# Two fused attention layers over eight images: units moved within layers, sums copied first at the end, and a copy given to another engine

## The chip, the cores and the metric

One core of one Trainium2 chip runs the kernel. The metric is the device time of one execution in microseconds (us); the figure for a kernel is the median of its runs. A profiled execution is one of its own, with a time of its own; its span is the stretch that the hardware profiler records.

The engines named below: TensorE (PE) multiplies matrices and writes into PSUM, VectorE (DVE) adds and multiplies element by element, ScalarE (ACT) computes exponentials and copies, GpSimd (POOL) does small work, and SyncE (SP) issues most DMAs. PSUM has eight banks; one bank holds 128 partitions by 512 floats here.

## The reference, cut to what matters

```python
# x: 8 images, 64 channels, 64 x 64 positions (n = 4096)
# layer 0
f = Wf @ x + bf            # 8 rows
g = Wg @ x + bg            # 8 rows
hh = Wh @ x + bh           # 64 rows
s = einsum('bci,bcj->bij', f, g)
o = einsum('bcj,bij->bci', hh, softmax(s, axis=2))
x = x + o
# layer 1
xn = group_norm(x, gamma, beta)            # 8 groups of 8 channels
q, k, v = split(w_qkv @ xn + b_qkv, 3)
attn = softmax(q.T @ k * 64 ** -0.5)
x = x + w_proj @ (attn @ v.T).T + b_proj
```

Both layers are full attention over 4096 positions, for each of eight images, in 32-bit floats.

## The kernel before, in words

**Tiling.** The 4096 positions of an image are taken as two halves of 2048, which lie on partitions 0 to 63 and 64 to 127. The queries of both halves are worked in four chunks of 512 columns (`NC`, `CW`). For each chunk the keys go by in 16 tiles (`NT`); one key tile of one chunk is a *step*. A step makes the scores of the queries against two groups of 128 keys, the exponentials of these, and two jobs on the exponentials: PE *weighs* the values with them, adding into an accumulator in PSUM, and DVE adds them up elementwise into `esum`, for the divisor of the softmax. In the trace those sums are the rows `TENSOR_TENSOR esum_l<-esum_l,e_l 128x2048`, or with `kq_l`, `vt_l` or `free` in the place of `esum_l` where the sum is kept elsewhere. The first sum of a chunk joins the tiles of the chunk's first two steps (`e_l,e_l`). The exponentials stand in a ring of seven buffers (`e`, `ppool`).

**Order of the layers.** `L0(0), L0(1), L1(0), L0(2), L1(1), ..., L0(7), L1(6), L1(7)`, where L0(b) is layer 0 of image b: layer 1 of an image runs after layer 0 of the next image. Layer 0 has scores of few rows (8 channels, split into a high and a low part), so it takes PE least of all against DVE; layer 1 needs more of PE.

**PSUM.** Banks 1 to 6 are three pairs for scores. Banks 0 and 7 are accumulators: layer 0 uses one of the two for a chunk, by turns (chunks 0 and 2 bank 0, chunks 1 and 3 bank 7), layer 1 both. In layer 0 PE goes in *rounds*: it scores six banks full, or seven when the accumulator that isn't in use is free (bank 0 is then the first of the seven, bank 7 the last), or two fewer when a pair is lent to a *unit*; ACT takes the exponentials, and PE meanwhile weighs the exponentials of the round before.

**Units.** All work beside scoring, weighing and summing is cut into units: projections (`project`, `project_direct`, `project_all`), values (`values`), normalisation (`normal`), and what follows a chunk (`finish`). `at_step(s, work, takes)` puts a unit down for step s, and `take` hands out those that are due, at most one at a time of those that need a pair of banks (`PAIR`) or a bank (`BANK`). The due steps of `before()` count from the start of the preceding layer 1, or for image 0's layer 1 from the start of layer 0 of image 1 (step 64, the `where` of line 861). So a unit of image 0's layer 1 with due step under 64 is done in layer 0 of image 1, and from 64 on in layer 1 of image 0 itself.

**When a chunk is done.** `finish` has its accumulator copied out of PSUM into `raw` by `total`: by one copy on ACT in layer 0 (L664); in layer 1 by two copies on ACT, or by a copy and a sum on DVE where layer 0 comes next. Then come, as units, `halves` (the sum of the two key groups of `esum`), `transposed` (the DVE reduction `part_l`), `reciprocals`, and `result` with `residual`. For chunks 0 to 2 of layer 0 of images 1 to 7 the sums are held until layer 1 of another image runs (`holds`). The very last chunk has its own ending, `end` (L434): the sums by PE into a bank, their reciprocal `rt` (L456), a copy of them `zs_end` (L458), the copy of one accumulator to `raw_end` (L460), the sum with the other, the check of all sums against `SUM_MIN` and `SUM_MAX` (`ok_end`, `bad`), the residual, and two stores of the output (L817). Were a sum of exponentials out of bounds, a general path would run; with these inputs it doesn't.

**Order on the engines.** Every matmul goes through `matmul` (L150, recorded at L151), which chains it behind the one before: PE's order is the order of the program. DVE's operations go through `InOrder` (L138, recorded at L141); they are chained only while `tight` is set, which is during the first eight chunks and in `end`. Otherwise the scheduler of the Tile framework places the operations of DVE and ACT. `behind` holds a unit until the latest sum of exponentials has been issued.

**The start.** `warm(ones, 18)` and `warm(wfg, 10)` give PE matmuls of no use while the first data come (L194, L236). The small weights WfT and WgT come by two DMAs each, by ACT's and SP's queue (L196 to L198), then x of image 0 by SP (L199); GpSimd's queue brings the biases, and GpSimd makes `lane` (iota), `fgb` and others. `project_direct` makes f and g of chunk 0, `project(0, (1,))` those of chunk 1, `project(1)` those of chunks 2 and 3: PE, then ACT adds the bias (`full`, L586), then DVE parts f and g into a high and a low part (`high`, `split`), then 8 or 16 small DMAs by SP lay the parts out on the partitions (L602).

Of the kernel before, what the change touches and what calls it, by code (L numbers as in the profile page):

```python
# [9 lines left out]
F32 = mybir.dt.float32  # L10
F32R = mybir.dt.float32r
# [8 lines left out]
CW = 512  # L20
P = 128
# [47 lines left out]
def fast_path(  # L69
# [125 lines left out]
    w1 = const.tile([P, 2, C8], F32, name="w1")  # L195
    for i, (w, queue) in enumerate(((WfT, nc.scalar), (WgT, nc.sync))):  # L196
        for h in range(2):
            queue.dma_start(w1[ts(h, C), i, :], w)  # L198
# [36 lines left out]
    wfg = wfg.rearrange("p i s c -> p (i s c)")  # L235
    warm(wfg, 10)  # L236
    fgb_low = const.tile([P, 2], F32, name="fgb_low")
# [95 lines left out]
    class Attention:  # L333
# [100 lines left out]
        def end(self, acc, esum, e, t):  # L434
# [18 lines left out]
            for p in range(2):  # L453
                self.weigh(acc, e[:, p], t, p, False, p == 1, slice(0, CW))
            rt = work.tile([P, width], F32, tag="zs", name="rt")
            vector.reciprocal(rt, z)  # L456
            zs = work.tile([P, width], F32, tag="zs", name="zs_end")
            nc.scalar.copy(zs, z)  # L458
            raw = work.tile([P, CW], F32, tag="raw", bufs=4, name="raw_end")
            nc.scalar.copy(raw, acc[0])  # L460
            vector.tensor_add(raw, acc[1], raw)
            for rows, (h, i) in zip(groups, parts):
                matmul(
                    laid[ts(h, C), i, :],
                    ident[rows, rows.start : rows.start + 1].broadcast_to([32, C]), rt[rows, :],
                    start=True, stop=True, tile_position=(rows.start, h * C),
                )
            by_half = raw.rearrange("p (i n) -> p i n", i=2)
            vector.tensor_mul(by_half, by_half, laid)
            for k in range(2):  # L470
# [7 lines left out]
                bad[:, 1:], dealt, SUM_MAX, ok, op0=ALU.is_le, op1=ALU.mult  # L478
            )
            for i in range(1 + QP):  # L480
                matmul(bad_ps, bad[:, i : i + 1], ones[:, 0:1], start=i == 0, stop=i == QP)
# [3 lines left out]
    class Layer0(Attention):  # L485
# [4 lines left out]
        def before(self):  # L490
# [3 lines left out]
            def begin():  # L494
# [78 lines left out]
        def project(self, k, js=(0, 1)):  # L573
# [4 lines left out]
            for j in js:  # L578
# [84 lines left out]
        def total(self, raw, acc, index):  # L663
            nc.scalar.copy(raw, acc[0])  # L664
            return None
# [6 lines left out]
    class Layer1(Attention):  # L672
# [8 lines left out]
        def before(self):  # L681
# [130 lines left out]
        def residual(self, o, c):  # L812
            vector.scalar_tensor_tensor(
                o, o, k1["pb"], x_tiles[self.b][:, ts(c, CW)], op0=ALU.add, op1=ALU.add
            )
            for h in range(2):
                nc.sync.dma_start(out[self.b, :, ds(h * NH + c * CW, CW)], o[ts(h, C), :])  # L817
            if c == NC - 1 and self.b + 3 < B:
                load_x(self.b + 3)
# [607 lines left out]
```

## Time and profile before

| | us |
|---|---|
| median of 10 runs | 2988.5 |
| lowest and highest of them | 2987.9, 2991.91 |
| the profiled execution | 2988.05 |
| its span | 2986.2 |
| PE's granted clock in the span, of full speed | 0.999 |

The profiled execution is 1.85 us longer than its span. By stretch of the trace, with the busy time of the three engines that matter:

| stretch (us from the start of the span) | what runs | PE | DVE | ACT |
|---|---|---|---|---|
| 545.5 to 691 | L0(2) | 145.09 | 139.68 | 122.02 |
| 691 to 914 | L1(1) | 223.00 | 182.30 | 135.86 |
| 914 to 1059 | L0(3) | 144.59 | 139.55 | 121.91 |

A busy time is the time in which an engine had some operation going. A line of the timeline gives the start of an operation, its length, the engine, the line of the code, and `out<-in` with the tile names; `x7` at its end says that seven alike were drawn together, and what stands in brackets is the idle time just before and who ended it. Line 141 is the helper for all of DVE's operations and line 151 that for all of PE's, so they are told apart by tile. In a row of the costliest groups, the numbers behind the bar are busy time, the mean of one in ns, and the idle time before them.

The end of the kernel, from the timeline: the sums are read by DVE's reciprocal first, then by ACT.

```profile
2974.30 1.76 DVE L141 RECIPROCAL rt<-banks 128x256 f32<-128x256 f32 x1 [0.81 <-PE banks L151]
...
2976.10 0.37 ACT L458 COPY zs_end<-banks 128x256 f32<-128x256 f32 x1 [3.86 <-DVE rt L141]
...
2976.37 0.59 ACT L460 COPY raw_end<-banks 128x512 f32<-128x512 f32 x1
...
2978.66 0.74 DVE L141 SCALAR_TENSOR_TENSOR raw_end<-raw_end,pb,x 128x512 f32<-128x512 f32 x1
```

### The profile page before, as it was taken

The numbers are of one execution on the slowest core, as the hardware profiler recorded it, in microseconds if no ns is written. First come the engines' busy times: TensorE is split into PE (matmuls) and PEld (weight loads), VectorE is DVE, ScalarE is ACT, GpSimd is POOL, SyncE is SP. The second block draws the span as 40 slices with busy tenths as digits, with TensorE's granted clock in tenths as the row PEclk, the third lists the DMA queues.
The fourth block names the chain that finished last, engine by engine and source line by source line (L and its number), as shares of the span: only waits on it lengthen the run. The fifth ranks groups of instructions, "written<-read, shape, count | busy, mean of one in ns | idle before, by whom it ended". The sixth has DMA issues, their size and how long they took to land.

```text
span 2986.2 us, 58391 instructions
## 1 busy us (share of the span) xinstructions
PE 2969.5 (99%) x25693; PEld 1080.6 (36%) x25693; DVE 2567.8 (86%) x1634; ACT 2072.4 (69%) x2019; POOL 16.1 (1%) x40
## 2 busy tenths in 40 slices
PE   9999999999999999999999999999999999999998
PEld 4333333333333333333333333333333333333333
DVE  7999986899869998799977999769997699976776
ACT  7888666786667866688556885568856688566554
POOL 2000000000000000000000000000000000000000
PEclk9999999999999999999999999999999999999999
DMA  2100101102001020010200002001020000010000
GB/s 66 44 8 15 45 19 23 26 1 48 18 21 26 1 51 16 21 25 1 52 17 23 22 1 52 20 19 22 1 52 19 20 8 1 17 26 12 9 16 13
DMA packets 77910, 66.97 MB, mean 22 GB/s; under 512 B 54816, under 2 KB 54848, under 8 KB 75856
## 3 DMA queue, kind: packets, MB, share of 16 engines
q1 hardware_dynamic: 76560, 63.04, 8.9%
q8 instruction: 203, 3.33, 0.5%
q14 instruction: 59, 0.48, 0.1%
q0 software_dynamic: 768, 0.09, 0.0%
q10 hardware_dynamic: 320, 0.04, 0.0%
HBM read 39.84 MB, written 12.32 MB: 17 GB/s over the span
## 4 chain that ended last, share of the span: by engine, by line
PE 95%; DVE 2%; issue 1%; ACT 1%; DMA 0%; SPq 0%; DVEq 0%; ACTq 0%
PE banks L151 95%; DVE vt_l L141 1%; DVE esum_l L141 1%; ACT e_l L1025 0%; DVE free L141 0%; DMA w<-in_WgT_dram 0%; DMA moments<-mv_l 0%; DMA group_l<-moments 0%; ACT kq_l L777 0%; SPq L700 0%; DVE rt L141 0%; DVE x L141 0%; DVE raw_l L141 0%; DVE raw_end L141 0%; DVE st_l L141 0%
## 5 line engine op out<-in xcount | busy, mean ns | idle before, releaser
L141 DVE TENSOR_TENSOR esum_l<-esum_l,e_l 128x2048 f32<-128x2048 f32 x601 | 1374.5, 2287 | 268.7 <-ACT e_l L984 246.1
L984 ACT ACTIVATE e_l<-banks 128x1024 f32<-128x1024 f32 x1024 | 992.3, 1022 | 681.1 <-PE banks L151 670.4
L151 PE MATMUL banks<-e_l,v_l 64*64 64x512 f32 (+1 forms) x8772 | 1090.1, 587 | 0.0
L1025 ACT ACTIVATE e_l<-banks 128x2048 f32<-128x2048 f32 (+3 forms) x728 | 952.8, 1372 | 171.6 <-PE banks L151 167.2
L151 PE MATMUL banks<-kq_l 64*64 64x512 f32 (+1 forms) x8448 | 1001.2, 585 | 0.5 <-ACT kq_l L777 0.5
L151 PE MATMUL banks<-e_l,vt_l 128*64 128x512 f32 (+1 forms) x4056 | 828.1, 549 | 0.0
L141 DVE TENSOR_TENSOR kq_l<-kq_l,e_l 128x2048 f32<-128x2048 f32 x252 | 577.4, 2291 | 24.7 <-ACT e_l L1025 0.9
L151 PEld LDWEIGHTS banks<-e_l,v_l 64*64 64x64 f32 (+1 forms) x8772 | 346.1, 133 | 590.1 <-issue 494.8
L151 PEld LDWEIGHTS banks<-kq_l 64*64 64x64 f32 (+1 forms) x8448 | 325.0, 134 | 594.9 <-issue 561.1
L151 PEld LDWEIGHTS banks<-e_l,vt_l 128*64 128x64 f32 x4056 | 267.5, 136 | 467.4 <-issue 447.4
L151 PE MATMUL banks<-fg_l 32*128 32x512 f32 x1792 | 202.9, 457 | 5.4 <-ACT e_l L1025 4.5
L141 DVE TENSOR_TENSOR esum_l<-e_l,e_l 128x2048 f32<-128x2048 f32 x43 | 97.7, 2272 | 83.9 <-ACT e_l L984 83.9
L151 PEld LDWEIGHTS banks<-fg_l 32*128 32x128 f32 x1792 | 84.2, 182 | 183.0 <-ACT e_l L1025 140.2
L141 DVE TRANSPOSE_TENSOR_REDUCE part_l<-esum_l 128x32 f32<-128x1024 f32 x38 | 74.9, 1971 | 0.0
L141 DVE TENSOR_TENSOR free<-free,e_l 128x2048 f32<-128x2048 f32 x28 | 64.2, 2291 | 2.6
L141 DVE TENSOR_TENSOR esum_l<-esum_l 128x1024 f32<-128x1024 f32 x38 | 46.3, 1219 | 0.2
L141 DVE TENSOR_TENSOR raw_l<-raw_l,r_l 128x512 f32<-128x512 f32 x63 | 43.2, 685 | 2.4 <-DMA r_l<-recips 2.4
L141 DVE TENSOR_TENSOR kq_l<-e_l,e_l 128x2048 f32<-128x2048 f32 x18 | 41.1, 2283 | 0.0
L664 ACT COPY raw_l<-banks 128x512 f32<-128x512 f32 x32 | 18.9, 590 | 24.4 <-PE banks L151 23.5
L141 DVE TRANSPOSE_TENSOR_REDUCE part_l<-kq_l 128x32 f32<-128x1024 f32 x18 | 35.2, 1958 | 0.0
L141 DVE TENSOR_TENSOR vt_l<-vt_l,e_l 128x2048 f32<-128x2048 f32 x14 | 32.1, 2291 | 1.2
L777 ACT ACTIVATE kq_l<-banks,kqb 64x256 f32<-64x256 f32 x64 | 30.1, 470 | 1.2
(134 smaller groups left out, 501.9 us busy)
## 6 DMA issues: line engine op xcount, KB each, us to landing
r_l<-recips SPq DMA_DIRECT2D x126, 128.0 KB
kq_l<-kq_l SPq DMA_DIRECT2D x64, 128.0 KB
out_dram<-raw_l SPq DMA_DIRECT2D x62, 128.0 KB
x<-in_x_dram SPq DMA_DIRECT2D x30, 256.0 KB
fg_l<-fg_sent_l SPq DMA_DIRECT2D x24, 256.0 KB
fg_l<-fg_sent_l SPq DMA_DIRECT2D x48, 128.0 KB
part_l<-part_l SPq DMA_DIRECT2D x236, 4.0 KB
fg_sent_l<-high_l SPq DMA_DIRECT2D x28, 128.0 KB
```

Source lines behind the costliest of these rows:

```text
L141: it = getattr(nc.vector, name)(*args, **kwargs)
L151: in_order(nc.tensor.matmul(*args, **kwargs))
L664: nc.scalar.copy(raw, acc[0])
L777: nc.scalar.activation(self.q[ts(h, C), cols[1]], ps[other, 1, 0:width], AF.Identity, bias=k1["kqb"][other, :],)
L984: nc.scalar.activation(e[:, p], both_ps[p], AF.Exp, scale=at.scale)
L1025: nc.scalar.activation(e.rearrange("k p h n -> k (p h) n")[:, first_ : first_ + n_, :], banks[:, bank : bank + n_, :], AF.Exp, scale=at.scale,
```

## The change

It has these parts:

1. WgT comes by GpSimd's queue in place of SP's, and the second warming has 6 matmuls, not 10.
2. `project` of layer 0 returns its second half (parting on DVE and the DMAs) as a function. For chunks 2 and 3 the projection stays at step 2, its parting becomes a unit of its own at step 4, and the loads of images 1 and 2 go with it; the values of chunks 2 and 3 come at steps 3 and 5, not 5 and 8.
3. Layer 1 of image 0: the four chunks are, counted from step 64, normalised at steps 40, 45, 50 and 55, projected at 48, 76, 92 and 104, and their values made at 53, 65, 69 and 73. Before, these were 27, 31 and 33 for the first chunk and eight more for each further one. So three of the four projections and three of the four value units come at due steps past 64. For the other images the steps stay as they were.
4. `end`: ACT copies the sums to `zs_end` first, and the reciprocal reads that copy; the matmuls and the two DVE operations of the check stand ahead of the sum of the two accumulators; the second of the last two stores goes by ACT's queue.
5. `total` of layer 0: for images 0 and 1 the accumulator is copied by ACT as before, for images 2 to 7 by DVE.

```diff
--- before.py
+++ after.py
@@ -193,7 +193,7 @@
 
     warm(ones, 18)
     w1 = const.tile([P, 2, C8], F32, name="w1")
-    for i, (w, queue) in enumerate(((WfT, nc.scalar), (WgT, nc.sync))):
+    for i, (w, queue) in enumerate(((WfT, nc.scalar), (WgT, nc.gpsimd))):
         for h in range(2):
             queue.dma_start(w1[ts(h, C), i, :], w)
     load_x(0, (0, 1, 2, 4))
@@ -233,7 +233,7 @@
         wfg = const.tile([P, 2, 4, C8], F32, name="wfg")
         nc.vector.tensor_copy(wfg, w1.unsqueeze(2).broadcast_to([P, 2, 4, C8]))
     wfg = wfg.rearrange("p i s c -> p (i s c)")
-    warm(wfg, 10)
+    warm(wfg, 6)
     fgb_low = const.tile([P, 2], F32, name="fgb_low")
     fgb, lowmask = fgb_low[:, 0:1], fgb_low[:, 1:2]
     for j in range(2):
@@ -452,31 +452,31 @@
                     )
             for p in range(2):
                 self.weigh(acc, e[:, p], t, p, False, p == 1, slice(0, CW))
-            rt = work.tile([P, width], F32, tag="zs", name="rt")
-            vector.reciprocal(rt, z)
             zs = work.tile([P, width], F32, tag="zs", name="zs_end")
             nc.scalar.copy(zs, z)
+            rt = work.tile([P, width], F32, tag="zs", name="rt")
+            vector.reciprocal(rt, zs)
             raw = work.tile([P, CW], F32, tag="raw", bufs=4, name="raw_end")
             nc.scalar.copy(raw, acc[0])
-            vector.tensor_add(raw, acc[1], raw)
+            for k in range(2):
+                matmul(
+                    dealt[:, ts(k, 4)], zs[:, ts(k, P)], ident[:, 0:P:32], start=True, stop=True
+                )
+
+            ok = small.tile([P, QP], F32, tag="zt", bufs=4, name="ok_end")
+            vector.tensor_scalar(ok, dealt, SUM_MIN, -1.0, op0=ALU.is_ge, op1=ALU.mult)
+            vector.scalar_tensor_tensor(
+                bad[:, 1:], dealt, SUM_MAX, ok, op0=ALU.is_le, op1=ALU.mult
+            )
             for rows, (h, i) in zip(groups, parts):
                 matmul(
                     laid[ts(h, C), i, :],
                     ident[rows, rows.start : rows.start + 1].broadcast_to([32, C]), rt[rows, :],
                     start=True, stop=True, tile_position=(rows.start, h * C),
                 )
+            vector.tensor_add(raw, acc[1], raw)
             by_half = raw.rearrange("p (i n) -> p i n", i=2)
             vector.tensor_mul(by_half, by_half, laid)
-            for k in range(2):
-                matmul(
-                    dealt[:, ts(k, 4)], zs[:, ts(k, P)], ident[:, 0:P:32], start=True, stop=True
-                )
-
-            ok = small.tile([P, QP], F32, tag="zt", bufs=4, name="ok_end")
-            vector.tensor_scalar(ok, dealt, SUM_MIN, -1.0, op0=ALU.is_ge, op1=ALU.mult)
-            vector.scalar_tensor_tensor(
-                bad[:, 1:], dealt, SUM_MAX, ok, op0=ALU.is_le, op1=ALU.mult
-            )
             for i in range(1 + QP):
                 matmul(bad_ps, bad[:, i : i + 1], ones[:, 0:1], start=i == 0, stop=i == QP)
             nc.scalar.copy(n_bad, bad_ps)
@@ -506,24 +506,27 @@
                     self.project_all()
                 else:
                     self.project_direct()
-                    self.project(0, (1,))
+                    self.project(0, (1,))()
 
             def rest():
-                self.project(1)
+                self.parted = self.project(1)
+
+            def parted():
+
+                self.parted()
                 with tc.issue_after(self.sent.ins):
                     for b in (1, 2):
                         load_x(b)
 
             if self.b == 0:
-                return [(-1, begin, True), (2, rest, True)] + [
+                return [(-1, begin, True), (2, rest, True), (4, parted, False)] + [
                     (
-                        (-1, 1, 5, 8)[c],
+                        (-1, 1, 3, 5)[c],
                         lambda c=c: self.values(x_tiles[0][:, ts(c, CW)], wh, c),
                         True,
                     )
                     for c in range(NC)
                 ]
-
 
 
             s, spread = (28, 32) if self.b == 1 else (0, 28)
@@ -584,25 +587,30 @@
             full = ppool.tile([P, 2, 2, CW], F32, tag="e", name=f"full_{n}")[:, 0]
             rows = slice(js[0] * C, P)
             nc.scalar.activation(full[rows], ps[rows], AF.Identity, bias=fgb[rows, :])
-            high = ppool.tile([P, 2, 2, CW], F32R, tag="e", name=f"high_{n}")[:, 0]
-            vector.tensor_copy(high[rows], full[rows])
-
-            split = high
-            vector.scalar_tensor_tensor(
-                split[rows], high[rows].bitcast(F32), lowmask[rows, :], full[rows],
-                op0=ALU.mult, op1=ALU.add,
-            )
-
-            for j in js:
-                cols = ts(2 * k + j, CW)
-                for h in range(2):
-                    for p in range(2):
-                        rows = ts(2 * h + p, 32)
-                        for i, (dst, half) in enumerate(((self.f, h), (self.g, p))):
-                            self.sent = nc.sync.dma_start(
-                                dst[rows, cols].bitcast(F32),
-                                split[ts(2 * j + i, 32), half, :].bitcast(F32),
-                            )
+            part = rows
+
+            def split():
+                high = ppool.tile([P, 2, 2, CW], F32R, tag="e", name=f"high_{n}")[:, 0]
+                vector.tensor_copy(high[part], full[part])
+
+                both_ = high
+                vector.scalar_tensor_tensor(
+                    both_[part], high[part].bitcast(F32), lowmask[part, :], full[part],
+                    op0=ALU.mult, op1=ALU.add,
+                )
+
+                for j in js:
+                    cols = ts(2 * k + j, CW)
+                    for h in range(2):
+                        for p in range(2):
+                            rows = ts(2 * h + p, 32)
+                            for i, (dst, half) in enumerate(((self.f, h), (self.g, p))):
+                                self.sent = nc.sync.dma_start(
+                                    dst[rows, cols].bitcast(F32),
+                                    both_[ts(2 * j + i, 32), half, :].bitcast(F32),
+                                )
+
+            return split
 
         def project_all(self):
 
@@ -661,7 +669,9 @@
                 )
 
         def total(self, raw, acc, index):
-            nc.scalar.copy(raw, acc[0])
+
+            copy = nc.scalar.copy if self.b < 2 else vector.tensor_copy
+            copy(raw, acc[0])
             return None
 
         def residual(self, o, c):
@@ -749,11 +759,17 @@
                 (at[2], behind(deviations), False),
             ]
             for c in range(NC):
-                s = 31 + 8 * c if self.b == 0 else 35 + 7 * c
+
+
+                at = (
+                    (40 + 5 * c, (48, 76, 92, 104)[c], (53, 65, 69, 73)[c])
+                    if self.b == 0
+                    else (31 + 7 * c, 35 + 7 * c, 37 + 7 * c)
+                )
                 units += [
-                    (s - 4, behind(lambda c=c: normal(c)), False),
-                    (s, lambda c=c: self.project(c), True),
-                    (s + 2, lambda c=c: self.values(self.x[:, ts(c, CW)], k1["wvp"], c), True),
+                    (at[0], behind(lambda c=c: normal(c)), False),
+                    (at[1], lambda c=c: self.project(c), True),
+                    (at[2], lambda c=c: self.values(self.x[:, ts(c, CW)], k1["wvp"], c), True),
                 ]
             return units
 
@@ -814,7 +830,8 @@
                 o, o, k1["pb"], x_tiles[self.b][:, ts(c, CW)], op0=ALU.add, op1=ALU.add
             )
             for h in range(2):
-                nc.sync.dma_start(out[self.b, :, ds(h * NH + c * CW, CW)], o[ts(h, C), :])
+                queue = nc.scalar if h and self.b == B - 1 and c == NC - 1 else nc.sync
+                queue.dma_start(out[self.b, :, ds(h * NH + c * CW, CW)], o[ts(h, C), :])
             if c == NC - 1 and self.b + 3 < B:
                 load_x(self.b + 3)
 
```

More of the change, by code (lines that the diff above doesn't have):

```diff
@@ L454, in end @@
                 self.weigh(acc, e[:, p], t, p, False, p == 1, slice(0, CW))
-            rt = work.tile([P, width], F32, tag="zs", name="rt")
-            vector.reciprocal(rt, z)
             zs = work.tile([P, width], F32, tag="zs", name="zs_end")
             nc.scalar.copy(zs, z)
+            rt = work.tile([P, width], F32, tag="zs", name="rt")
+            vector.reciprocal(rt, zs)
             raw = work.tile([P, CW], F32, tag="raw", bufs=4, name="raw_end")
             nc.scalar.copy(raw, acc[0])
-            vector.tensor_add(raw, acc[1], raw)
-            for rows, (h, i) in zip(groups, parts):
-                matmul(
-                    laid[ts(h, C), i, :],
-                    ident[rows, rows.start : rows.start + 1].broadcast_to([32, C]), rt[rows, :],
-                    start=True, stop=True, tile_position=(rows.start, h * C),
-                )
-            by_half = raw.rearrange("p (i n) -> p i n", i=2)
-            vector.tensor_mul(by_half, by_half, laid)
             for k in range(2):
@@ L479, in end @@
             )
+            for rows, (h, i) in zip(groups, parts):
+                matmul(
+                    laid[ts(h, C), i, :],
+                    ident[rows, rows.start : rows.start + 1].broadcast_to([32, C]), rt[rows, :],
+                    start=True, stop=True, tile_position=(rows.start, h * C),
+                )
+            vector.tensor_add(raw, acc[1], raw)
+            by_half = raw.rearrange("p (i n) -> p i n", i=2)
+            vector.tensor_mul(by_half, by_half, laid)
             for i in range(1 + QP):
```

## The prediction

> **What bounds the kernel now.** I read the page first, then what TensorE (PE) waited for, then the busy time by stretch, then the timelines of VectorE (DVE), ScalarE (ACT) and PE at the places that the diff touches.
>
> ```profile
> PE 2969.5 (99%) x25693; PEld 1080.6 (36%) x25693; DVE 2567.8 (86%) x1634; ACT 2072.4 (69%) x2019; POOL 16.1 (1%) x40
> ```
>
> PE is busy for 2969.5 of 2986.2 us: whatever makes it wait is added to the time, and little can be gained by taking waits away. Its waits (engine, line, releaser: us, times, longest):
>
> ```profile
> PE banks L151 <- ACT e_l L1025: 4.5, 8, 1.3
> PE banks L151 <- DVE bad L141: 1.4, 1, 1.4
> PE banks L151 <- DVE kq_l L141: 1.2, 1, 1.2
> ```
>
> PE never waits for the copy of a finished accumulator in layer 0. But in layer 0 DVE is nearly full. The columns are stretch, length, then busy time of PE, PEld, DVE, ACT, POOL:
>
> ```profile
> 949.00:984.00 35.00, 35.00 (x211) 12.51 (x210) 33.55 (x16) 29.79 (x24) 0.00 (x0) 1.00 0.02 3
> 984.00:1019.00 35.00, 35.00 (x215) 12.45 (x213) 33.55 (x16) 29.99 (x24) 0.00 (x0) 1.00 0.00 1
> ```
>
> 33.55 us is the sum of its operations; between two dependent sums there is a bubble of 0.1 us, so there is no free time. DVE runs behind. Image 3 at the end of its chunk 0 (start, length):
>
> ```profile
> 953.23 0.59 ACT L664 COPY raw_l<-banks 128x512 f32<-128x512 f32 x1
> ...
> 956.39 2.28 DVE L141 TENSOR_TENSOR kq_l<-e_l,e_l 128x2048 f32<-128x2048 f32 x1
> ...
> 957.17 0.74 PE L151 MATMUL banks<-fg_l 32*128 32x512 f32 x7
> ...
> 958.78 2.29 DVE L141 TENSOR_TENSOR kq_l<-kq_l,e_l 128x2048 f32<-128x2048 f32 x1
> ```
>
> ACT empties the accumulator's bank at 953.23 to 953.82. At 957.17 PE begins a round of seven score matmuls; the freed bank is the first of the seven. DVE starts chunk 1's first sum only at 956.39. At the end of chunk 3, where layer 1 of image 2 begins:
>
> ```profile
> 1058.36 0.59 ACT L664 COPY raw_l<-banks 128x512 f32<-128x512 f32 x1 [3.42 <-PE banks L151]
> ...
> 1061.73 1.90 PE L151 MATMUL banks<-e_l,v_l 64*64 64x512 f32 x16
> ...
> 1063.63 0.69 DVE L141 CAST high_l<-full_l 128x1024 fp32r<-128x1024 f32 x1
> 1064.23 1.22 DVE L141 TENSOR_TENSOR kq_l<-kq_l 128x1024 f32<-128x1024 f32 x1
> 1065.37 1.28 DVE L141 SCALAR_TENSOR_TENSOR high_l<-high_l,lowmask,full_l 128x1024 fp32r<-128x1024 f32 x1
> 1066.57 1.91 DVE L141 TRANSPOSE_TENSOR_REDUCE part_l<-kq_l 128x32 f32<-128x1024 f32 x1
> 1068.41 2.24 DVE L141 TENSOR_TENSOR esum_l<-e_l,e_l 128x2048 f32<-128x2048 f32 x1
> ```
>
> PE needs bank 7 at 1061.73, for the first weighing of layer 1. DVE ends its last sum of that chunk at 1063.72, 1.99 us later, and the reduction at 1068.48. This lag costs nothing before, since PE asks DVE for nothing here.
>
> **What the Trainium skill says.** (1) "PSUM — Partial Sum Buffer", section "PSUM bank collisions raise a hardware error": PE's writing and another engine's reading of one bank must be separated by a semaphore, by bank. The trace agrees: the bank copied at 953.23 is written again from 957.17. So the wait of PE goes wherever the copy goes. (2) "TensorE: Matmul & The Clock Gate", section "What's actually happening": PE falls to half its clock after an idle window of 3.4 us, which runs freely, and needs a busy window to come back. The trace shows the cold start (36 records in 3.85 us, then 20 in 1.38) and no long gap later, so for the middle of the kernel no run here shows it. (3) "DMA: Bandwidth & Descriptors", section "Latency and other measured facts": first byte about 1 us by GpSimd's queue, 0.6 us by the hardware queues. In the trace GpSimd's bias DMA landed 3.0 us after its issue; the second WgT DMA by SP took 3.24.
>
> **The change, part by part.**
>
> *Layer 0's accumulator copies, images 2 to 7: from ACT to DVE* (`total`). 24 copies leave ACT, where PE waited for none of them: gain 0. On DVE a copy of this shape costs 682 ns, by this row (six of them at other places):
>
> ```profile
> L141 DVE COPY raw_l<-banks 128x512 f32<-128x512 f32 x6 | 4.1, 682 | 0.0
> ```
>
> The built program of the change shows where they stand. In chunks 0 to 2 the copy stands behind the next chunk's first sum. In chunk 3 it stands behind everything shown above up to the reduction (in image 7, behind halves and reduction). And PE waits for each: the round of seven for the first three, the first weighing of layer 1 for the last.
>
> How far one inserted copy shifts DVE: an independent operation starts 0.09 us before the end of the one ahead (1063.63 against 1063.72), on both sides of the copy, and the bubble of 0.10 before the next dependent sum (958.67 to 958.78) vanishes: 0.68 - 0.09 - 0.09 - 0.10 = 0.40 us. From the end of the operation ahead to the copy's end it is 0.68 - 0.09 = 0.59, and PE starts 0.06 after DVE ends (233.71 to 233.76, a projection).
>
> Image 3, first boundary: sum ends 958.67, copy 959.26, PE 959.32 instead of 957.17: 2.15 us. Second: 994.42 + 0.40 + 0.59 + 0.06 = 995.47; here the freed bank is 7, the last of the seven, due at 990.95 + 0.33 + 2.15 = 993.43: 2.04 more, 4.19 in all. Third: 1030.17 + 0.80 + 0.65 = 1031.62, before PE gets there (1028.74 + 4.19 = 1032.93): nothing. Seam to layer 1: 1068.48 + 3 x 0.40 + 0.59 + 0.06 = 1070.33 instead of 1061.73: 8.60 us in all, 4.41 of it here. DVE doesn't starve in between: its sums start 3.4 to 8 us after their exps end in layer 0 past the first chunk, and PE's delay relative to DVE's is at most 4.19 - 0.80 = 3.39, in a stretch where that slack is near 5.
>
> So an image costs (reduction's end - first weighing's start) + 1.85. The six differences: 700.43 - 693.23 = 7.20; 1068.48 - 1061.73 = 6.75; 1437.39 - 1430.24 = 7.15; 1805.50 - 1798.74 = 6.76; 2174.00 - 2167.23 = 6.77; 2541.19 - 2534.72 = 6.47. Sum 41.1, plus 6 x 1.85: **+52.2 us**. Layer 1 can't give it back: PE is full there, by matmuls alone. Behind the waiting matmul stand all others of PE, and ACT's exps behind those.
>
> *Image 0's projections.* Three of four projections and three of four value units leave layer 0 of image 1 for layer 1 of image 0. In the built program PE has 309 score rounds, not 311. A round of five to seven costs 0.66 us and 0.16 for changing over (a round of seven takes about 3.82 us, of which 3.0 are weighing): 1.6. Changing tile shapes costs about 0.11 less at each of the six in layer 1: 0.7. The waits for kq_l (1.21 on DVE at 233.76, 0.48 on ACT at 237.99) go. That would be 4.0. But at 236.00 and 255.42 ACT's exp starts 0.09 us after the sum that frees its buffer: DVE is next in line there, and is relieved by two normalisations only (2 x 0.46). I take 0.9 up to there and 1.6 behind: **-2.5**, between -1 and -4.
>
> *Start.* WgT by GpSimd: two issues of 0.67 and 0.53 from 1.36; landing 3.0 after issue, by the bias row, gives 4.95 against 4.73 by SP. Four warm matmuls less (8 records of 58 ns) save 0.46: the direct projection starts at about 6.18, not 6.51. x starts 1.5 us earlier, and isn't late before either. The biases and the iota queue behind the two issues, about 1.15 later: bias lands at 5.4, so the table load (1.28) ends at 6.8; ACT needs it at 7.3. If the issues took 0.5 longer each, this cover would be gone and up to 0.5 lost. **-0.3** (-0.5 to +0.5).
>
> *First sum ahead of the parting, values at 3 and 5.* The 16 DMAs of chunks 2 and 3 leave about 1.2 us later (sum 2.29, less the wait for e), the first eight land near 27; the ninth key tile is scored after 31. Hidden; so are the x loads behind them. The rounds before 21 us, with 3.0 us of waits, are cut otherwise: 0, -1 to +1.
>
> *End.* ACT copies the sums first (0.37), then the reciprocal (1.76) runs from 2974.75 to 2976.5 instead of 2976.07. The check is drawn ahead of the sum of the accumulators (0.35), and the raw copy comes 0.2 earlier: residual at about 2979.3 against 2979.40. The two stores:
>
> ```profile
> 2979.43 1.11 SPq L817 DMA_DIRECT2D out_dram<-raw_end  x2
> ```
>
> now start together, which saves 0.55. What follows is a fixed row of waits: **-0.65** (-1.2 to 0; a reciprocal from SBUF isn't in the trace, I take the same time).
>
> **Sum.** 52.2 - 2.5 - 0.3 - 0.65 = +48.7 on the profiled execution of 2988.05 (span 2986.2 plus 1.85): 3036.8. The median is 0.45 above it: 3037 us, 1.6% slower.
>
> **Rivals.**
> - *Clock.* Each seam leaves PE idle for about 4 us. A free window of 3.4 fits whole with a chance of some 0.18, by the skill's figure; one hit costs 1.7 to 3.4, an estimate. If nearly all seams hit: 3037 + 6 x 2.5 = 3052. Against: gaps of 2 us at the other boundaries are too short.
> - *Only DVE's own time counts.* If lag were absorbed and each copy put its 0.68 on the path: 24 x 0.68 = 16.3, less 3.5: 3001. For it: DVE has some idle time at an image's start. Against: the lag shown is already there when PE asks.
> - *Not slower.* If DVE's copies at the seam ended before PE needs the bank, nothing is left but the gains: 2985, or 2981 with them at their high end. It decides at a lag of DVE behind PE's first weighing of -1.85 us; the trace shows +6.5 to +7.2. For it: only that DVE's order could be different from the program's, and in the trace it never is.
>
> **Numbers.** Forecast 0.82, clock 0.06, DVE's own time 0.06, not slower 0.06. The forecast's own range: each inserted copy may shift DVE by 0.2 to 0.72 (-4 to +6), gains may be 1 higher or lower in each part, one or two clock hits add 5: 3028 to 3048. To leave out no more than 2 in 10 with the clock rival within: 3024 to 3054. A measurement of this kernel can tell about 0.2% (6 us) from no change. Faster by more: 0.03 (the last rival's high end); within: 0.03; slower: 0.94.
>
> **What would show it.** Right: new waits of PE on DVE raw_l, about 18 of them, 2 us at the ends of chunks 0 and 1 and over 4 us at layer 1's start, for images 2 to 7; none at chunk 2; no wait on kq_l near 234; layer 0 of these images about 8.7 us longer each, layer 1 as long as before. Wrong: PE without such waits, or waits at chunk 2 (then DVE's shift is larger than 0.40), or matmuls of layer 1 at twice their pitch behind a seam (clock).

## The result, and the profile after

| | us |
|---|---|
| before, median of 28 runs | 2988.49 (2987.9 to 2992.06) |
| changed, median of 8 runs | 3044.57 (3042.33 to 3049.66) |
| ratio, 95% interval | 1.0186 (1.0177 to 1.0195) |
| changed, the profiled execution | 3047.2, span 3045.5 |

The change makes the kernel 1.9% slower, 56 us. The profiled execution is 59.3 us longer in its span (from first to last instruction) than that of before, and this difference is divided up below.

The page's first part, and then the largest of PE's waits (engine, line, releaser: us in total, times, longest), of the changed kernel:

```profile
PE 2991.8 (98%) x25685; PEld 1401.3 (46%) x25685; DVE 2583.1 (85%) x1658; ACT 2061.5 (68%) x1990; POOL 17.4 (1%) x42
```

```profile
PE banks L151 <- DVE raw_l L141: 38.0, 17, 3.2
```

This wait is new: PE now waits 17 times for a copy on DVE, 38.0 us in all. It accounts for 38 of 59 us only, and PE's own busy time has grown by 22.3 us (2969.5 to 2991.8) with almost the same instructions. So a part of the loss isn't idle time but slower matmuls. (PE's weight loads, PEld, are busier too, 1401.3 us against 1080.6. That is so in every kernel below that has the copy of chunk 3 on DVE, and in no other; why is open. It costs nothing here: behind its first chunk layer 1 is as long as before, within 0.01 us a chunk.) Both parts can be seen where layer 1 of image 2 begins. Such a place, where a layer 0 ends and a layer 1 begins, is called a *seam* here. The timelines of DVE and PE there, one after the other (start, length):

```profile
1076.58 0.69 DVE L141 CAST high_l<-full_l 128x1024 fp32r<-128x1024 f32 x1
1077.18 1.22 DVE L141 TENSOR_TENSOR kq_l<-kq_l 128x1024 f32<-128x1024 f32 x1
1078.32 1.28 DVE L141 SCALAR_TENSOR_TENSOR high_l<-high_l,lowmask,full_l 128x1024 fp32r<-128x1024 f32 x1
1079.52 1.90 DVE L141 TRANSPOSE_TENSOR_REDUCE part_l<-kq_l 128x32 f32<-128x1024 f32 x1
1081.33 0.65 DVE L141 COPY raw_l<-banks 128x512 f32<-128x512 f32 x1
```

```profile
1078.65 1.03 PE L151 MATMUL banks<-e_l,v_l 64*64 64x512 f32 x4
1082.04 1.99 PE L151 MATMUL banks<-e_l,v_l 64*64 64x512 f32 x8 [2.36 <-DVE raw_l L141]
```

PE weighs into bank 0 at 1078.65 and then stands until DVE's copy of bank 7 ends at 1081.98. The next eight records of matmuls take 1.99 us, where eight of the same size took 1.04 just before (those from 1077.79 on). The busy time by stretch around this place (stretch, length, then PE, PEld, DVE, ACT, POOL, PE's granted clock, DMA share, GB/s) says why:

```profile
1078.57:1081.98 3.41, 1.11 (x8) 0.15 (x2) 3.41 (x4) 1.52 (x2) 0.00 (x0) 1.00 0.28 65
1081.98:1085.40 3.42, 3.36 (x16) 1.07 (x19) 2.20 (x2) 0.00 (x0) 0.00 (x0) 0.50 0.45 92
1085.40:1088.81 3.41, 3.41 (x36) 1.41 (x32) 0.29 (x1) 1.94 (x2) 0.00 (x0) 1.00 0.57 143
```

For 3.41 us after the wait the granted clock is 0.50, and PE does 16 records of matmuls in place of 36. A half-clock stretch of this length, called a *window* below, costs 1.7 us, half of it, when PE is busy throughout; longer stretches are whole multiples of it. The trace after has nine of them between 13 and 2222 us, the trace before none (the first warming up, and what lies behind PE's last matmul, apart). Nine times 1.7 are some 15 of the 22.3 us. Most of the rest lies at the waits, where PE still counts as busy with the last matmuls ahead: at image 7's seam, without a half-clock stretch, PE is delayed by 3.64 us but idle for 2.58 only.

Where the 59.3 us come from, by the starts of the first exponential of each chunk in both traces. The row of an image goes from the start of its layer 0 to the start of the next image's layer 0, and so takes in the seam behind it; that of image 7 ends with the first chunk of L1(6):

| part | predicted | measured | half-clock stretches in it |
|---|---|---|---|
| start and chunk 0 of image 0 | -0.3 | +2.18 | 1 |
| image 0's moved units (L0(1), L1(0)) | -2.5 | -2.36 | 0 |
| copies of image 2 | 9.05 | 11.12 | 2 |
| image 3 | 8.60 | 11.05 | 2 |
| image 4 | 9.00 | 10.48 | 2 |
| image 5 | 8.61 | 10.26 | 1 |
| image 6 | 8.62 | 10.27 | 1 |
| image 7 | 8.32 | 7.93 | 0 |
| end | -0.65 | -1.6 | |
| sum | +48.7 | +59.3 | 9 |

Images 5 and 6 have one stretch each, at the seam, and lie 1.65 above the forecast; image 7 has none and lies 0.4 below it, which isn't explained.

### The profile page after: what moved, and what is told of

Read it like the earlier page. It is cut to its first block, busy times and chain, and to the rows that moved or that the text cites. A ratio compares the mean times of both kernels' runs of the same rounds, so it can differ in the third digit from the quotient of the medians.

```text
span 3045.5 us, 58370 instructions
## 1 busy us (share of the span) xinstructions
PE 2991.8 (98%) x25685; PEld 1401.3 (46%) x25685; DVE 2583.1 (85%) x1658; ACT 2061.5 (68%) x1990; POOL 17.4 (1%) x42
## 4 chain that ended last, share of the span: by engine, by line
PE 72%; DVE 23%; issue 3%; ACT 1%; DVEq 0%; DMA 0%; POOL 0%; ACTq 0%; POOLq 0%
PE banks L151 72%; DVE kq_l L141 12%; DVE esum_l L141 8%; DVE vt_l L141 1%; DVE raw_l L141 1%; ACT e_l L1042 1%; DVE free L141 1%; ACT e_l L1001 0%; DVE part_l L141 0%; DVE high_l L141 0%; DVEq L141 0%; DMA w<-in_WgT_dram 0%; DMA fg_l<-high_l 0%; DVE fg_l L141 0%; DVE x L141 0%
## 5 line engine op out<-in xcount | busy, mean ns | idle before, releaser
L151 PE MATMUL banks<-e_l,v_l 64*64 64x512 f32 (+2 forms) x8772 | 1309.0, 589 | 16.6 <-DVE raw_l L141 16.6
L151 PE MATMUL banks<-kq_l 64*64 64x512 f32 (+1 forms) x8448 | 1214.3, 587 | 1.8 <-ACT e_l L1042 1.4
L151 PEld LDWEIGHTS banks<-e_l,v_l 64*64 64x64 f32 (+1 forms) x8772 | 560.9, 134 | 471.5 <-issue 335.7
L151 PEld LDWEIGHTS banks<-kq_l 64*64 64x64 f32 (+1 forms) x8448 | 527.6, 135 | 443.3 <-issue 302.9
L151 PEld LDWEIGHTS banks<-wkq_wvp,kq_l 64*64 64x64 f32 x1024 | 28.1, 134 | 10.6 <-issue 4.3
L151 PEld LDWEIGHTS banks<-wh,x 64*64 64x64 f32 x1024 | 26.8, 134 | 11.2 <-issue 7.0
```

The costliest lines, as they stand in the source:

```text
L151: in_order(nc.tensor.matmul(*args, **kwargs))
```

## The experiments

**All copies on ACT again.** The whole of the rest of the change stays.

```diff
-            copy = nc.scalar.copy if self.b < 2 else vector.tensor_copy
-            copy(raw, acc[0])
+            nc.scalar.copy(raw, acc[0])
```

> The changed kernel with layer 0's accumulator copies of all images on ACT again; all else of the change stays. Theory: the whole loss is PE waiting for DVE's copies (with TensorE at half clock for one window of 3.41 us after some of these waits), and the other parts bring -2.4 us (image 0's units), about -1.5 (end) and +0.4 (start), or up to +2.1 at the start in executions where a half-clock window falls there: 2985 to 2987 us. Rival, the moved units or the new start cost something too: 2990 us or more.

Measured: 2984.5 us median of 19 runs, 0.9986 of before (0.9979 to 0.9993), half a us under what was expected. The copies are the whole loss: all the rest together is a gain of about 4 us. By the starts of chunks, the moved units of image 0 bring -1.08 and -1.57 in L0(1) and -2.32 at its end, and give back 1.83, 0.43 and 0.43 in L1(0): -2.28.

**DVE's time without PE's wait.** All copies on ACT, and the same time spent on DVE.

```diff
-            copy = nc.scalar.copy if self.b < 2 else vector.tensor_copy
-            copy(raw, acc[0])
+            nc.scalar.copy(raw, acc[0])
+            if self.b >= 2:
+                vector.tensor_tensor(raw, raw, raw, op=ALU.max)
```

> All accumulator copies on ACT, but for images 2 to 7 DVE does an extra elementwise operation of the same size on each copied tile in SBUF (a maximum of the tile with itself, which changes nothing), at the same places in its order. DVE is as busy as in the changed kernel, but PE waits for none of it. Theory: DVE's time as such is hidden: within 1 us of the kernel with all copies on ACT, 2985 to 2988 us. Rival, DVE's own 0.68 us for each of 24 copies is what counts: 16 us more, 3001 us.

Measured: 2984.36 us, 0.9986 (0.9979 to 0.9993), against 2984.5 without the extra operations. In this trace's list for the tile `raw_l`, the 24 operations have a median of 684 ns:

```profile
L141 DVE TENSOR_TENSOR raw_l<-raw_l x24: 652/684/694, 590.6 to 2542.8; 128x512 f32<-128x512 f32 x24
```

They are as long as the copies, they stand at the same places of DVE's order (between the same two operations, in all 24 cases), and they cost nothing. DVE being busy isn't what counts; that PE waits for it is.

**Chunks 0 to 2 alone, and chunk 3 alone.** Two kernels, one line each:

```diff
+            copy = nc.scalar.copy if self.b < 2 or index % NC == NC - 1 else vector.tensor_copy
...
+            copy = nc.scalar.copy if self.b < 2 or index % NC < NC - 1 else vector.tensor_copy
```

> Only chunks 0 to 2 are copied by DVE for images 2 to 7; chunk 3 by ACT. Theory (PE meets a lag of DVE that builds up over layer 0, and pays each part of it once): 2.15 + 2.04 us an image, 25 us in all, and 0 to 5 half-clock windows of 1.7 us: 3011 to 3019 us, with no wait at the start of layer 1. Rival, each copy costs its own share: 18/24 of the loss, 3029 us.

> Only chunk 3 is copied by DVE for images 2 to 7; chunks 0 to 2 by ACT. Theory: with nothing paid before, PE pays DVE's whole lag at the start of layer 1: the six differences of the trace before, 41.1 us, plus 6 x 0.65 for the copy, 45 us, and about five half-clock windows of 1.7 us: 3036 to 3041 us. Then chunks 0 to 2 alone and chunk 3 alone add up to more than both together (70 against 52 without the clock). Rival, each copy costs its own share: 6/24 of the loss, 3000 us.

Measured: 3019.02 us for chunks 0 to 2 (ratio 1.0099, 1.0084 to 1.0115), 3045.14 us for chunk 3 alone (1.0183, 1.0167 to 1.0199). Above 2984.5 that is 34.5 and 60.6, and both together are 60.1 in the changed kernel. Six copies on chunk 3 cost as much as all 24. A copy has no price of its own: PE pays DVE's lag, and pays each part of it once, early or late. That the two sums come out so nearly the same is in part chance: the lag alone is 45.0 us by the trace before for chunk 3 and 52.2 for all copies, and the clock makes up more of the cost with chunk 3 alone.

With chunks 0 to 2 there is no wait at the start of layer 1, as expected; its trace has ten waits for DVE's copies, 18.6 us in all, and six half-clock stretches, one more than the expectation allowed. Both kernels are at or beyond the upper end of what was expected, chunk 3 by 4 us, and its trace shows the rest, first in PE's waits, then in PE's timeline and in the busy time by stretch at image 3's seam:

```profile
PE banks L151 <- DVE raw_l L141: 38.0, 6, 6.7
```

```profile
1079.31 2.82 PE L151 MATMUL banks<-e_l,v_l 64*64 64x512 f32 x10 [6.67 <-DVE raw_l L141]
```

```profile
1074.78:1085.02 10.24, 5.71 (x28) 1.93 (x32) 6.68 (x5) 0.26 (x1) 0.00 (x0) 0.50 0.37 86
```

The clock falls within the wait of 6.67 us and stays at half up to 1085.02, 5.71 us after PE is busy again at 1079.31. At half speed those 5.71 us cost some 2.9; the expectation had put 1.7 us on each seam for this.

**Keeping PE busy in the wait.** The kernel with chunk 3 alone on DVE, with scores computed again into a pair of banks that is free, ahead of the matmul that waits; their results are overwritten by the scores that follow.

```diff
             for m in range(2):
+                if m and seam:
+                    for _ in range(13):
+                        self.scores(pairs[(turn + 1) % 3], 0, 0, 0)
                 for h in range(2):
...
+        seam = at.kind == 1 and c == 0 and j == 0 and 1 <= at.b <= 6
         at.weigh(acc, e[:, p], t, p, j == 0, j == 2 * NT - 1, cols)
```

> The kernel in which DVE copies chunk 3 alone, with 52 matmuls of no use (scores computed again into a free pair of banks) put ahead of the matmul that waits, six times: 5.6 us of PE's work in a wait of 5.7 to 6.7 us. Theory: after an idle wait TensorE runs at half clock until the end of the next windows, and that is 15 of the 60 us lost; with PE kept busy the clock stays whole: 3029 to 3032 us. Rival, the clock is a side matter and the wait alone is the cost: no change, 3045 us.

Measured: 3051.63 us, 1.0213 (1.0198 to 1.0229), neither of the two. The fill was mis-sized: each matmul leaves two records, and 52 of them take 11.2 us, so every seam became 11.20 us longer, and PE waited for no DVE copy any more. The same with six repeats in place of 13:

> As the filled kernel before it, with 24 matmuls of no use in place of 52, six times. The trace of that one showed that the 52 took 11.2 us, not 5.6, and so more than the wait; 24 take 5.15 us and fit into the wait of 5.7 to 6.7 us. Theory: PE isn't idle long enough for a half-clock window, the copy on DVE ends the wait as before, and what the clock took goes: 2984.5 plus 45, 3029 to 3032 us. Rival, the clock is a side matter and DVE's wait alone is the cost: 3045 us.

Measured: 3031.82 us, 1.0142 (1.0127 to 1.0158): 13.3 us less than without the fill (3045.14), though DVE's copies and their places are the same and PE does 144 matmuls more. The seam in its trace, where PE's helper stands at L152 (timeline of PE, then the busy time by stretch):

```profile
1070.76 5.70 PE L152 MATMUL banks<-kq_l 64*64 64x512 f32 x46
1077.99 1.50 PE L152 MATMUL banks<-e_l,v_l 64*64 64x512 f32 x10 [1.53 <-DVE raw_l L142]
```

```profile
1070.76:1078.00 7.24, 5.71 (x54) 2.00 (x46) 7.24 (x7) 0.96 (x2) 0.00 (x0) 1.00 0.15 33
1078.00:1085.00 7.00, 7.00 (x68) 2.96 (x72) 4.32 (x2) 2.66 (x3) 0.00 (x0) 1.00 0.44 98
```

The wait still ends with DVE's copy, at 1077.99, but the ten records behind it take 1.50 us, not 2.82, and the clock is whole. Between 20 us and PE's last matmul there is no half-clock stretch in this trace. The six seams now cost 7.42, 7.75, 7.40, 7.42, 7.75 and 6.77, together 44.5 us, where the sum from the trace before had said 45.0 for the lag alone; in the trace without the fill they cost 60.9. So the loss of this kernel is the lag and the half clock, and the two have been parted. In the changed kernel itself, with its shorter waits, no fill was tried; there the division rests on the table above.

**The copy straight behind its chunk's last sum.** The number of DVE copies stays; the order changes, and the layer 0 projections of images 3 to 7, each of which stood ahead of the last copy of the image before, come a step later.

```diff
+            nonlocal added
+            if self.b < 2:
+                nc.scalar.copy(raw, acc[0])
+            else:
+                copied = vector.tensor_copy(raw, acc[0])
+                in_order(copied, "copies")
+                added = copied.ins
...
-            added = vector.tensor_add(esum, first if t == 1 else esum, e).ins
+            sum_ = vector.tensor_add(esum, first if t == 1 else esum, e)
+            added = sum_.ins
+            if t in (1, NT - 1) and not tight:
+                in_order(sum_, "copies")
...
-            s, spread = (28, 32) if self.b == 1 else (0, 28)
+            s, spread = (28, 32) if self.b == 1 else (0 if self.b == 2 else 1, 28)
```

In `project_all` the two DVE operations are also put behind `added`.

> The changed kernel, but each DVE copy of layer 0 is put straight behind the last sum of its chunk, ahead of the next chunk's first sum, and the projection that stood ahead of the last copy comes a step later. The copies and their number stay. Theory: what counts is where DVE stands when it gets to the copy. From the trace before, each copy then shifts DVE by 0.59 us, the first one isn't waited for, and an image costs 4.4 to 5.8 us: 28.5 us over the 2984.5 us of the kernel with all copies on ACT, so 3013 us, and up to 3023 us with half-clock windows of 1.7 us. Rival, a copy on DVE costs the same wherever it stands: 3044 us.

Measured: 3018.09 us, 1.0099 (1.0084 to 1.0115), within what was expected. 26.5 us of the 60.1 go by the order, with the same copies on the same engine. PE's waits for DVE's copies are 11, with 15.8 us in all, none at the end of chunk 0 but for 0.24 us in two images. Each copy now stands directly behind its chunk's last sum, so what is left is DVE's lag behind PE at that sum itself, and four half-clock windows.

**The start.** The executions of the kernel with all copies on ACT lie at two levels, ten at 2983.9 to 2984.5 and nine at 2985.9 to 2987.5 us. Its profiled execution is one of the latter; its busy time by stretch there:

```profile
9.04:12.45 3.41, 1.75 (x62) 1.26 (x58) 3.24 (x5) 2.91 (x3) 3.37 (x7) 1.00 0.03 5
12.45:19.28 6.83, 6.11 (x20) 1.36 (x20) 2.49 (x2) 4.13 (x4) 6.72 (x15) 0.50 0.34 89
```

In a stretch of 3.41 us PE is idle for 1.66, while it waits for the first two rounds of scores, and for two such stretches its clock is halved. That is one execution of the upper level; there is no trace of the lower. The next kernel fills these waits with more of the warming matmuls:

```diff
+            if i == 0 and group[0][0][:2] == (0, 0):
+                warm(wfg, 6)
+            elif i == 0 and group[0][0][:2] == (0, 1):
+                warm(wfg, 8)
             for (k, t, p, h), bank in group:
```

> The kernel with all copies on ACT, with 6 and 8 more warming matmuls in the waits of 0.93 and 1.27 us ahead of the first and the second round of scores. Theory: the two levels of the runs, 2984.2 and 2986 to 2987.5, come from a window with enough idle time at 9 to 14 us, after which TensorE runs at half clock for one or two windows; filled, the upper level goes: all runs 2983.8 to 2984.8 us. Rival, the upper level has another cause: the same two levels.

Measured: 2983.86 to 2985.03 us in 21 runs, median 2984.34 (0.9985, 0.9978 to 0.9991). The upper level is gone. (The kernel before has two levels as well, near 2988.2 and 2991.5 us. Its one trace is of the lower, so what makes the upper one is open.) But the median is hardly lower than 2984.5, and chunk 0 of image 0 is still 0.59 us longer in its trace than before the change. One part of the change was left to suspect, the first sum ahead of the parting:

```diff
-                self.parted = self.project(1)
+                self.project(1)()
+                with tc.issue_after(self.sent.ins):
+                    for b in (1, 2):
+                        load_x(b)
...
-                return [(-1, begin, True), (2, rest, True), (4, parted, False)] + [
+                return [(-1, begin, True), (2, rest, True)] + [
                     (
-                        (-1, 1, 3, 5)[c],
+                        (-1, 1, 5, 8)[c],
```

> The kernel with all copies on ACT and the warming matmuls in the first waits, with the second part of the change undone: chunks 2 and 3 of image 0 are parted at once, ahead of the first sum, and the values come at steps 5 and 8. Theory: the other cutting of the first rounds is what makes chunk 0 of image 0 0.59 us longer than before: chunk 0 gets that back, 2983.7 us. Rival, the first sum ahead of the parting is a gain that something else in the start takes back: 2985 us or more.

Measured: 2983.82 us median of 19 runs, 0.9981 of before (0.9974 to 0.9988), and chunk 0 takes 37.15 us as before (37.14), against 37.73 with the part. So that part costs 0.59 us where nothing was expected; three more traces with the part and no half clock in that chunk have 0.59 or 0.60 too. The place of the parting, that of the loads and the steps of the values were undone together, so which of them costs it is open. This kernel, which has the change's other parts without the copies on DVE and with the filled waits, has the lowest median of all, though its interval overlaps with that of the one above.

**The end.** All copies on ACT, both last stores by SP:

```diff
-                queue = nc.scalar if h and self.b == B - 1 and c == NC - 1 else nc.sync
-                queue.dma_start(out[self.b, :, ds(h * NH + c * CW, CW)], o[ts(h, C), :])
+                nc.sync.dma_start(out[self.b, :, ds(h * NH + c * CW, CW)], o[ts(h, C), :])
```

> The kernel with all copies on ACT, but with both of the last two stores by SP's queue, as before the change. One look at the end of the trace. Theory: the second queue brings 0.55 us, the issue of a store. Rival: it brings nearly all of the 1.5 us that the end became shorter, since two descriptors' completions are waited for in turn.

Measured, in a single execution (2988.3 us, with two half-clock windows at the start): from the start of the last weighing to the end of the span 11.18 us, against 10.51 with two queues (in the trace of the kernel with filled waits at the start) and 12.02 before. The second queue brings 0.67, the sum of the last operations up to the residual 0.17. The remaining 0.67 of the 1.5 lies between the residual and the end with the same two stores on the same queue; a single execution doesn't say whether it belongs to the change.

## Why the prediction was right, and where its sum was short

*Right: the mechanism.* "So the wait of PE goes wherever the copy goes", and the cost of an image as the difference between DVE's reduction and PE's first weighing plus 1.85. The median was forecast at 3037 and is 3044.57, 7.6 above and within 3028 to 3048. The waits are where they were put: at the ends of chunks 0 and 1 and at the seam, none at chunk 2, 17 of some 18 (the one that is missing is the second of image 4, where PE came late from a half-clock stretch). At image 3's first boundary DVE's sum ends at 969.62 in the trace after, the copy runs to 970.22, and PE starts:

```profile
970.28 0.73 PE L151 MATMUL banks<-fg_l 32*128 32x512 f32 x7 [2.08 <-DVE raw_l L141]
```

The shift there is 2.14 against 2.15 predicted, and 2.15 (once 2.16) and 2.14, against 2.15 and 2.04, at the two boundaries of images 5 to 7, which have no half-clock stretch there. That a copy alone costs nothing, that the lag is paid once and that the order decides was argued before and is shown by the four kernels above.

*Mis-sized: the wait at the seam.* "Each seam leaves PE idle for about 4 us", and over 4 us at layer 1's start as a sign of being right: the six waits there are 1.99, 2.36, 3.22, 3.23, 3.23 and 2.58 us. The delay itself is 3.64 to 6.00 us there, where 4.13 to 4.86 follow from the forecast; but PE counts as busy in a part of it, and in images 2 and 3 it came late already.

*Mis-sized: the clock.* The step was "Each seam leaves PE idle for about 4 us. A free window of 3.4 fits whole with a chance of some 0.18", and from it "one or two clock hits add 5"; and among the reasons against, "gaps of 2 us at the other boundaries are too short". A sign that the prediction had named for being wrong, matmuls of layer 1 at twice their pitch behind a seam, is there (1.99 us for eight records against 1.04). Eight stretches came in images 2 to 7 in the profiled execution, five at the seams and three behind waits of about 2 us. The sum for the copies was 52.2, the measured 61.1; five stretches at the seams at 1.71 us are 8.5 of the 8.9 between. The three at the other boundaries cost little more in the end, since PE comes later to the next wait and waits less: image 4 has 4.21 + 0.45 us at its two, against 2.15 + 2.14 in images 5 to 7; images 2 and 3 have 6.36 and 5.97 at theirs, and wait less at the seam for it. The rival with the clock had the right thing, and 0.06 was too little for it; it went too far in the price of a hit (2.5 us). There is some luck in the range: without the 5 us put in for one or two hits it would have ended at 3043, under the median measured. The filled kernel shows what the clock is worth where the waits are longest.

The Trainium skill's page "TensorE: Matmul & The Clock Gate", section "What's actually happening", was read as a window that must be idle throughout. The length of the stretch, 3.41 us, and that it runs freely, agree with it (the stretches at 703.11, 1081.98 and 1460.86 are whole multiples of 3.413 apart). That the window must be idle throughout is not what the traces show: the stretch at 1006.89 follows a window with 1.65 us idle of 3.41.

*Close: image 0's units.* -2.28 to -2.36 against -2.5. The waits for kq_l at 233.76 and 237.99 are gone as foreseen, and DVE was next in line as foreseen too: in the trace after PE waits at 239.44 and 243.81, 1.11 and 0.27 us, for exponentials, and the one ahead of the second had itself waited for a sum of DVE's.

```profile
242.73 1.94 ACT L1042 ACTIVATE e_l<-banks 128x1024 f32<-128x1024 f32 x2 [0.52 <-DVE free L141]
...
243.81 0.49 PE L151 MATMUL banks<-kq_l 32*128 32x512 f32 x2 [0.27 <-ACT e_l L1042]
```

In all L0(1) became some 5 us shorter (4.97 with all copies on ACT), and L1(0) gave 2.69 back, where the projections and values now are. The prediction had summed this up as a net gain only; how its 0.9 and 1.6 divide isn't shown by this.

*Wrong in small things.* The start was put at -0.3. In the kernel with filled waits, whose clock came up at 4.57 us, about as early as before (4.49), the first exponential is indeed 0.26 earlier; in the profiled execution of the changed kernel the clock came up at 6.79, and it is 0.41 later. The other 1.78 of the 2.18 arise in chunk 0: 0.59 by the second part of the change, the rest with the half-clock stretch at 13.61. "Hidden; so are the x loads behind them", said of the first sum ahead of the parting and the values at 3 and 5: PE waits for no load, but the part costs 0.59 us, which was put at 0, -1 to +1. The end was put at -0.65, -1.2 to 0, and is -1.5 to -1.6: 0.17 us for the operations up to the residual, where the prediction had 0.10, 0.67 for the second queue, where it had 0.55, and 0.67 behind the residual that it didn't have and that stays unexplained.

*The rivals.* "Only DVE's own time counts" gave 16.3 us for 24 copies and fell: they cost nothing when PE doesn't wait for them. "Not slower" would have needed another order on DVE; the earliest order that was tried still costs 33.6 us over the kernel with the copies on ACT.

## What to carry to other kernels

Before work is moved from one engine to another, look not at how busy the new engine is but at how far behind the waiting engine it runs at that moment; a full engine that nobody waits for may run many microseconds late at no cost, and the first thing that is put behind its queue collects the whole lag. An operation that frees a buffer belongs to an engine that is early, or straight behind what makes it possible. Price a new wait of TensorE with the clock too: of the waits at the ends of chunks, up to 2.44 us long, 3 of 11 in the changed kernel and 6 of 10 with chunks 0 to 2 alone were followed by 3.41 us at half clock. In the kernel with chunk 3 alone, with its waits of 5.7 to 6.7 us, useless matmuls put into the wait took the half clock away; in the waits of 2 us this wasn't tried.

## What the runs showed of the hardware that was not expected

- TensorE's clock went to half after windows of 3.41 us in which PE was idle for only about half of the time: 1.65 us of 3.41 ahead of 1006.89 in the trace after, and 1.66 ahead of 12.45 in that of all copies on ACT. Laid back from each trace's own changes of clock, the windows of all twelve traces say where the edge lies (from the first full clock to PE's last matmul, with PE's idle time as the trace counts it). Of the windows at full clock, none of more than 10,000 with up to 1.6 us of PE idle was followed by half clock, and all 14 with more than 2.02 us were. Of the 19 between, 15 were: the edge isn't sharp by this measure (the window from 1332.56 to 1335.97 with chunks 0 to 2 on DVE, 2.02 us idle, was followed by full clock). Whether the kind of matmul in the window counts stays open.
- The way back asks for more. Of the windows at half clock, all 28 with up to 0.14 us of PE idle were followed by full clock, none of the 13 with 0.5 us or more, and one of the four between. So the half clock lasted one window where PE was busy at once, two at the start of the kernel with all copies on ACT (0.72 us idle in the first), and three, 10.24 us, behind a wait of 6.67 us.
- The windows lie differently against the program in each execution, so the same program has more or fewer such stretches. That is what the spread of the kernel with all copies on ACT came from, 3.6 us, which shrank to 1.2 us once the first waits were filled.
